# Products of zeros in TensorE's thinly filled steps of a selective scan

## The chip, the cores and the metric

The kernel runs on one core of one Trainium2 chip. Its time is the device time of one execution in microseconds (us); the figure that counts is the median of several runs. One further execution is recorded by the hardware profiler, and all views below are of that one.

## The reference

Four layers work on four images of 64 x 64 positions with 96 channels. Layers 0 and 1 are selective scans over the image, layers 2 and 3 are attention without softmax and a quantized feed-forward block. Nearly all the time goes into layers 0 and 1. There, after a group norm, an input projection and a depthwise 3 x 3 convolution, the 192 inner channels are read in K = 4 orders, and for each order and each of N = 16 states a recurrence runs along the 4096 positions:

```python
def step(h, inp):
    u_t, dt_t, B_t, C_t = inp
    h = jnp.exp(dt_t[..., None] * A) * h + (dt_t * u_t)[..., None] * B_t[:, :, None, :]
    y = jnp.einsum('bkdn,bkn->bkd', h, C_t)
    return (h, y)
```

The sums over the 16 states, plus a skip term, are added up over the four orders; a layer norm, a gate and an output projection follow.

## The kernel before

**Tiling.** Two images are worked on at a time. A *phase* is one layer for one pair of images, four in all. A phase has 16 *blocks* (four reading orders, four parts of TB = 1024 positions each). A block has 48 *tiles*: two groups `g`, three parts `j` of 64 channels, and eight steps `n` in each group. That is 3072 tiles. Tile `n` belongs to image `n % 2` and holds two neighbouring states of it, one in each half of the 128 partitions, for 64 channels and 1024 positions. So the 16 values of `n` are eight pairs of states for each of the two images.

**The order of the work.** For PE, DVE, ACT and POOL the order of the instructions is the order in which the program writes them (`manual_schedule`). A loop over steps `i` writes, in each step, pieces of several tiles, so that the engines work on neighbouring tiles at once. Only the queue of transfers on SP is ordered by the framework's planner. The loop's heart is:

```python
if 0 <= i - 3 < end and tiles[i - 3][3] % GN == GN - 1:
    flush(i - 3)
if 0 <= i - 2 < end and tiles[i - 2][3] % 2:
    gather(i - 2)
if 0 <= i + 2 < end:
    row(i + 2)
if 0 <= i < end:
    scan(i)
```

**The parts of a tile** (lines of the profile before):

- `begin` (L652): POOL multiplies `du` with a row of B that was copied to all partitions, for the five states of `POOL_N`. For the other states, ACT takes the exponential of the decay (L669) here.
- `row` (L662): for the states outside `POOL_N`, PE writes the row of B to all partitions of a PSUM tile `psB`, as two products of 128 x 512 in bf16. There are two `psB` buffers.
- `product` (L676): DVE multiplies `psB` with `du`.
- `scan` (L684): DVE runs the recurrence over 1024 positions.
- `weigh` (L695): POOL multiplies the states with a row of C.
- `gather` (L727): in every second step PE adds two tiles (one of each image) into the sum over states `psY`; the operand `fold` adds the two halves of partitions. These are four fp32 products of 64 x 512, each of which is two matmuls in the records.
- `resume` (L718): at the first tile of a group of eight, PE puts the earlier sum (or the skip term) into `psY`; it opens the sum. The last gather of the group closes it, and `flush` (L739, L743) copies it out on ACT.

There is one `psY` tile, and six `flow` buffers `f` that hold decays and then weighted states.

**Beside the scan.** In the same loop, `advance()` takes the next piece of other work: the convolution of the coming phase (`conv_pieces`, L289 on PE), the norm, gate and projection of the phase just done (`tail_pieces`, L360 to L442), and the preparation of the next block (L543, L565, L569). These use two small PSUM tiles `psM`. After the last tile, layers 2 and 3 follow.

Of the kernel before, what the change touches and what calls it, by code (L numbers as in the profile page):

```python
# [15 lines left out]
C = 96  # L16
# [11 lines left out]
NG = 2  # L28
GN = N // NG
MANUAL = {mybir.EngineType.PE, mybir.EngineType.DVE, mybir.EngineType.Activation, mybir.EngineType.Pool}  # L30
POOL_N = (1, 4, 7, 10, 13)


@with_exitstack
def kernel(ctx: ExitStack, tc: tile.TileContext, ins, out, layers=(0, 1, 2, 3)):
# [72 lines left out]

    minus = wp.tile([96, 2 * N], BF16, tag="minus", name="minus")
    nc.vector.tensor_scalar_mul(minus, m32[0:96], -1.0)  # L110


    def per_channel(name, cols, src, tag):
# [98 lines left out]
    def conv_pieces(w, xin, xc, zg, done):  # L212

        norms = []

        def part_of(n):
            xb = wide([C, T], "xb")
            nc.sync.dma_start(xb, xin[n // NT][:, n % NT * T : (n % NT + 1) * T])
            return xb

        xbs = [part_of(n) for n in range(3)]
        yield False
        yield False
        for i in range(2):
            stats = small([C, NT, 6], "gst")
            for t in range(NT):
                if t:
                    yield False
                nc.vector.bn_stats(stats[:, t, :], xbs.pop(0))
                if i * NT + t + 3 < 2 * NT:  # L230
                    xbs.append(part_of(i * NT + t + 3))
            mv = small([C, 2], "gmv")
            nc.vector.bn_aggr(mv, stats)
            yield False
            pm = psM([C, 1])
            nc.tensor.matmul(pm, gmat, mv[:, 0:1], start=True, stop=True)
            yield True
            mean = small([C, 1], "gmean")
            nc.vector.tensor_copy(mean, pm)
            dev = small([C, 1], "gdev")  # L240
            nc.vector.tensor_sub(dev, mv[:, 0:1], mean)
            nc.vector.tensor_mul(dev, dev, dev)
            nc.vector.tensor_add(dev, dev, mv[:, 1:2])
            yield False
            pv = psM([C, 1])
            nc.tensor.matmul(pv, gmat, dev, start=True, stop=True)
            yield True
            t = small([C, 1], "grs")
            nc.vector.tensor_scalar_add(t, pv, 1e-5)
            scale = small([C, 1], f"gscale{i}")  # L250
            nc.gpsimd.tensor_tensor(scale, t, mhalf[0:C, 0:1], ALU.pow)
            yield False
            shift = small([C, 1], f"gshift{i}")
            nc.vector.scalar_tensor_tensor(shift, mean, -1.0, scale, ALU.mult, ALU.mult)
            norms.append((scale, shift))
        if "join" in w:
            w.pop("join")()
        rows = T // HW

        def load(t):  # L260
            pads = []
            for i in range(2):
                r0, r1 = t * rows - 1, (t + 1) * rows + 1
                lo, hi = max(r0, 0), min(r1, HW)
                pad = wide([C, rows + 2, HW + 2], "pad")
                nc.vector.memset(pad[:, :, 0:1], 0.0)
                nc.vector.memset(pad[:, :, HW + 1 : HW + 2], 0.0)
                if lo > r0:
                    nc.vector.memset(pad[:, 0, 1 : HW + 1], 0.0)
                if hi < r1:  # L270
                    nc.vector.memset(pad[:, rows + 1, 1 : HW + 1], 0.0)
                inner = pad[:, lo - r0 : hi - r0, 1 : HW + 1]
                nc.sync.dma_start(inner, xin[i][:, lo * HW : hi * HW].rearrange("p (r c) -> p r c", c=HW))
                pads.append((pad, inner))
            return pads

        done.append(now[0])
        coming = load(0)
        for t in range(NT):
            pads, coming = coming, None  # L280
            yield False
            for i in range(2):
                nc.scalar.activation(pads[i][1], pads[i][1], AF.Identity, bias=norms[i][1], scale=norms[i][0])  # L283
            yield False
            for j in range(J):
                px = psM([128, T])
                for tap in range(9):
                    for i in range(2):
                        nc.tensor.matmul(  # L289
                            px[64 * i : 64 * i + 64], w["wf"][:, tap, 64 * j : 64 * j + 64],  # L290
                            pads[i][0][:, tap // 3 : tap // 3 + rows, tap % 3 : tap % 3 + HW],
                            start=(tap == 0), stop=(tap == 8),
                        )
                    yield MORE if tap < 8 else True
                xo = thin([128, T], "xo")
                nc.scalar.activation(xo, px, AF.Silu, bias=w["cb"][:, j, :])
                pz = psM([128, T])
                for i in range(2):
                    nc.tensor.matmul(
                        pz[64 * i : 64 * i + 64], w["wz"][:, 64 * j : 64 * j + 64],  # L300
                        pads[i][0][:, 1 : 1 + rows, 1 : 1 + HW], start=True, stop=True,
                    )
                zo = thin([128, T], "zo")
                nc.scalar.activation(zo, pz, AF.Silu)
                nc.sync.dma_start(xc[:, j, t * T : (t + 1) * T], xo)
                nc.sync.dma_start(zg[:, j, t * T : (t + 1) * T], zo)
                if j == J - 1 and t + 1 < NT:
                    coming = load(t + 1)
                if j == J - 1:
                    done[0] += 1  # L310
                yield False

    def tail_pieces(w, units, y, zg, xin, xout, tokens):
# [11 lines left out]
        for t in units:  # L325
# [31 lines left out]
            for q in range(2):  # L357
                pt = psM([128, 2, D])
                for j in range(J):
                    nc.tensor.matmul(  # L360
                        pt[:, :, 64 * j : 64 * j + 64], yu[:, j, q * 128 : (q + 1) * 128], ident, start=True, stop=True
                    )
                if q:
                    statistics(0, pts)
                pts = pt
                yield True
# [50 lines left out]
            if tokens:  # L417
                xo = thin([128, 2, 2, C], "xn")
                pos = []
                for i in range(2):  # L420
                    half = slice(64 * i, 64 * i + 64)
                    pos.append(psM([128, 2, 128]))
                    for q in range(2):
                        tok = slice(q * 128, (q + 1) * 128)
                        o = pos[i][:, q, 0:C]
                        nc.tensor.matmul(o, xr[:, i, tok], ident[0:C, 0:C], start=True, stop=False)
                        for j in range(J):
                            nc.tensor.matmul(o, zu[half, j, tok], w["ow"][half, j, :], start=False, stop=(j == J - 1))  # L428
                    yield True
                for i in range(2):  # L430
                    nc.scalar.copy(xo[:, i], pos[i][:, :, 0:C])
# [2 lines left out]
            else:  # L434
                xo = thin([C, 2, U], "xn")
                pos = []
                for i in range(2):
                    half = slice(64 * i, 64 * i + 64)
                    pos.append(psM([C, U]))
                    nc.tensor.matmul(pos[i], ident[0:C, 0:C], xr[:, i, :], start=True, stop=False)  # L440
                    for j in range(J):
                        nc.tensor.matmul(pos[i], w["ow"][half, j, :], zu[half, j, :], start=False, stop=(j == J - 1))  # L442
                    yield True
                for i in range(2):
                    nc.scalar.copy(xo[:, i, :], pos[i])
# [55 lines left out]
    def prepare(ph, k, t):  # L501
# [38 lines left out]
        def project(s, j):  # L540
            if j == 0:
                pps.append(psM([76, T]))
            nc.tensor.matmul(  # L543
                pps[s], order[0][0][:, j, :], xs[j][:, halves[s]], start=(j == 0), stop=(j == J - 1)
            )

# [14 lines left out]
        def take(s, q):  # L561
            of = taken[s] = psM([2 * N, T])
            part = slice(0, 32 * q + 32)
            nc.tensor.matmul(of, ident[0 : 2 * N, 0 : 2 * N], rests[s][0 : 2 * N], start=True, stop=False)
            nc.tensor.matmul(of, minus[part], p["parts"][part, halves[s]], start=False, stop=True)  # L565

        def steps(s, j):
            pds.append(psM([128, T]))
            nc.tensor.matmul(  # L569
                pds[-1], order[0][1][64:76, j, :], rests[s][64:76], start=True, stop=True  # L570
            )

# [84 lines left out]
    def row(i):  # L657
        at, g, j, n = tiles[i]
        if n not in POOL_N:
            for s in range(2):  # L660
                ss = slice(s * T, (s + 1) * T)
                nc.tensor.matmul(  # L662
                    scanned[i][0][:, ss], sel[:, n, :], made[at]["parts"][:, ss], start=True, stop=True
                )

# [40 lines left out]
    def resume(i):  # L706
# [8 lines left out]
            parts = [(py[:, s * T : (s + 1) * T], old[:, s * T : (s + 1) * T]) for s in range(2)]  # L715
        banks = len(parts) * T // TB
        for m, (o, v) in enumerate(parts):
            nc.tensor.matmul(o, of, v, start=(m % banks == 0), stop=False)  # L718

    def gather(i):  # L720
        at, g, j, n = tiles[i]
# [2 lines left out]
        for s in range(2):  # L724
            ss = slice(s * T, (s + 1) * T)
            for e in range(2):
                nc.tensor.matmul(  # L727
                    py[64 * e : 64 * e + 64, ss], fold, two[e][:, ss],
                    start=False, stop=(n == g * GN + GN - 1),
                )  # L730

    def flush(i):

# [284 lines left out]
    with tc.manual_schedule(engines=MANUAL):  # L1018
# [27 lines left out]
        for i in range(-9, end + 4):  # L1046
# [7 lines left out]
                flush(i - 3)  # L1054
            if 0 <= i - 2 < end and tiles[i - 2][3] % 2:
                gather(i - 2)
            if 0 <= i + 2 < end:
                row(i + 2)
            if 0 <= i < end:
# [152 lines left out]
```

## Time and profile before

| what | value |
|---|---|
| median of three runs | 11160.67 us |
| lowest, highest | 11153.93, 11168.22 us |
| the profiled execution's own time | 11149.85 us |
| its span, first to last instruction | 11148.1 us |
| its mean granted clock of TensorE | 0.87 |
| 40 slices, each | about 279 us |

PE is TensorE's matmuls and PEld its weight loads; DVE is VectorE, ACT is ScalarE, POOL is GpSimd, and SP holds the queue of transfers. In the page's groups, the columns after the bar are the busy time of the group in us, the mean of one instruction in ns, and the engine's idle time just before these instructions, with what ended most of it. In the list of waits, a line says who waited for whom, for how many us in total, how often, and the longest. The clock is given in tenths in the slices and as a share in the tables of stretches. A line of the timeline gives start and duration in us, engine, line, operation, tiles and count, and in brackets the idle time before it with what ended it.

### The profile page before, as it was taken

Reading aid. Unit: us, or ns where it says so; the run is one execution under the profiler, and the core shown is the slowest. Engines: PE = TensorE matmul, PEld = TensorE weight load, DVE = VectorE, ACT = ScalarE, POOL = GpSimd, SP = SyncE. Lnnn points to the kernel's source line nnn. Section 1 sums busy time; section 2 is a strip of 40 time slices with the busy share of each in tenths; the row PEclk is TensorE's granted clock in tenths of the full one; section 3 lists DMA queues with packets and bytes.
Section 4 is the critical chain, followed back from the end, with each engine's and each line's share of the span. In section 5 each row is a group of like instructions: output and inputs, shape, how many; then the busy total and the mean of one; then the engine's idle time right before and its main releaser. Section 6 shows DMA issues by size and latency. Waiting matters only on the chain. (4 is left out here: it accounts for less than half of the span.)

```text
span 11148.1 us, 101994 instructions
## 1 busy us (share of the span) xinstructions
PE 8910.0 (80%) x30112; PEld 2880.5 (26%) x30112; DVE 9926.4 (89%) x6431; ACT 6423.1 (58%) x10575; POOL 10204.6 (92%) x5102
## 2 busy tenths in 40 slices
PE   7978888777777779887788878887778877778777
PEld 2222222111222212221222222222222322222365
DVE  3898999999999889989999999999999999999846
ACT  3656556554566646665566656665466655555576
POOL 3989999999999889999999999999999999999846
PEclk8989999888888889998888889998888888888877
DMA  5679976897578885798666656665556565556410
GB/s 134 158 141 162 141 160 157 145 134 136 149 171 151 140 151 149 157 159 132 138 169 157 157 146 169 164 159 143 149 157 156 155 149 148 143 137 159 122 33 22
DMA packets 1848188, 1604.57 MB, mean 144 GB/s; under 512 B 1412298, under 2 KB 1482892, under 8 KB 1847628
## 3 DMA queue, kind: packets, MB, share of 16 engines
q1 hardware_dynamic: 1847628, 1598.04, 66.1%
q8 instruction: 237, 3.88, 0.2%
q14 instruction: 323, 2.65, 0.1%
HBM read 1008.37 MB, written 186.65 MB: 107 GB/s over the span
## 5 line engine op out<-in xcount | busy, mean ns | idle before, releaser
L695 POOL TENSOR_TENSOR f<-f,crep 128x1024 f32<-128x1024 f32 x3072 | 7158.9, 2354 | 395.9 <-DVE f L684 296.6
L727 PE MATMUL psY<-f,fold 128*64 128x512 f32 x12288 | 3795.1, 698 | 183.4 <-POOL f L695 182.8
L684 DVE TENSOR_TENSOR_SCAN f<-f,state,psB 128x1024 f32<-128x1024 f32 x1584 | 3717.8, 2347 | 206.2 <-ACT f L669 50.1
L669 ACT ACTIVATE f<-delta,L_a 128x1024 f32<-128x1024 f32 x2112 | 2406.5, 1145 | 903.9 <-PE psY L727 829.8
L676 DVE TENSOR_TENSOR psB<-psB,du 128x1024 f32<-128x1024 f32 x2112 | 2558.9, 1212 | 362.9 <-PE psB L662 322.1
L662 PE MATMUL psB<-spB,sel 96*128 96x512 bf16 x4224 | 1387.8, 414 | 1613.5 <-DVE f L684 1599.0
L652 POOL TENSOR_TENSOR f<-du,brep 128x1024 f32<-128x1024 f32 x960 | 2265.7, 2360 | 127.2 <-PE psY L727 29.4
L684 DVE TENSOR_TENSOR_SCAN f<-psB,state,f 128x1024 f32<-128x1024 f32 x720 | 1676.7, 2329 | 76.8 <-POOL f L652 50.3
L727 PEld LDWEIGHTS psY<-f,fold 128*64 128x64 f32 x12288 | 974.9, 154 | 2525.3 <-issue 1806.8
L690 ACT COPY state<-f 128x1 f32<-128x1 f32 x2304 | 429.7, 188 | 2065.8 <-DVE f L684 2056.7
L669 ACT ACTIVATE psB<-delta,L_a 128x1024 f32<-128x1024 f32 x960 | 1070.2, 1115 | 696.0 <-DVE f L684 636.1
L684 DVE TENSOR_TENSOR_SCAN f<-f,psB 128x1024 f32<-128x1024 f32 x528 | 1208.3, 2288 | 57.6 <-ACT f L669 5.9
L662 PEld LDWEIGHTS <-sel 96*128 96x128 bf16 x4224 | 271.3, 99 | 3320.4 <-DVE f L684 2163.7
L289 PE MATMUL psM<-pad,wf 96*64 96x512 f32 x3456 | 901.4, 623 | 36.0 <-ACT pad L283 28.9
L684 DVE TENSOR_TENSOR_SCAN f<-psB,f 128x1024 f32<-128x1024 f32 x240 | 545.6, 2273 | 102.9 <-ACT psB L669 60.0
L718 PE MATMUL psY<-ysum,ident 128*128 128x512 f32 x768 | 554.5, 862 | 98.3 <-ACT ynew L743 86.7
L585 POOL TENSOR_TENSOR xs<-delta,xs 128x1024 f32<-128x1024 f32 x192 | 452.7, 2358 | 95.0 <-ACT delta L582 95.0
L569 PE MATMUL psM<-proj,dtw 12*128 12x512 f32 x768 | 455.2, 686 | 0.0
L543 PE MATMUL psM<-xs,xp 128*76 128x512 f32 x768 | 414.7, 651 | 5.5 <-DMA xs<-xcd 4.2
L718 PE MATMUL psY<-yold,ident 128*128 128x512 f32 (+2 forms) x960 | 370.6, 526 | 42.2 <-ACT ysum L739 26.7
L289 PEld LDWEIGHTS psM<-pad,wf 96*64 96x64 f32 x3456 | 221.4, 138 | 501.0 <-issue 422.6
L743 ACT COPY ynew<-psY 128x1024 f32<-128x1024 f32 (+2 forms) x312 | 242.4, 818 | 171.5 <-PE psY L727 171.5
(149 smaller groups left out, 6644.6 us busy)
## 6 DMA issues: line engine op xcount, KB each, us to landing
crep<-bc SPq DMA_DIRECT2D x2048, 256.0 KB, 4.8
delta<-delta SPq DMA_DIRECT2D x768, 256.0 KB, 4.8
du<-xs SPq DMA_DIRECT2D x768, 256.0 KB, 6.2
brep<-bc SPq DMA_DIRECT2D x640, 256.0 KB, 4.9
yd<-ynew SPq DMA_DIRECT2D x192, 512.0 KB, 7.8
xraw<-xcd SPq DMA_DIRECT2D x144, 512.0 KB, 8.5
yold<-yd SPq DMA_DIRECT2D x144, 512.0 KB, 8.9
xcd<-xo SPq DMA_DIRECT2D x96, 256.0 KB, 3.0
```

The costliest lines, as they stand in the source:

```text
L289: nc.tensor.matmul(px[64 * i : 64 * i + 64], w["wf"][:, tap, 64 * j : 64 * j + 64], pads[i][0][:, tap // 3 : tap // 3 + rows, tap % 3 : ta ...
L569: nc.tensor.matmul(pds[-1], order[0][1][64:76, j, :], rests[s][64:76], start=True, stop=True)
L585: nc.gpsimd.tensor_mul(xs[j], deltas[j], xs[j])
L652: nc.gpsimd.tensor_mul(f[:, 1:], made[at]["dus"][j][n % 2], reps[at, 0, n])
L662: nc.tensor.matmul(scanned[i][0][:, ss], sel[:, n, :], made[at]["parts"][:, ss], start=True, stop=True)
L669: nc.scalar.activation(out, made[at]["deltas"][j][n % 2], AF.Exp, scale=W[phases[ph][0]]["a"][:, k, j, n // 2 : n // 2 + 1])
L676: nc.vector.tensor_mul(scanned[i][0], scanned[i][0], made[at]["dus"][j][n % 2])
L684: nc.vector.tensor_tensor_scan(f[:, 1:], a, bu, 0.0 if t == 0 else states[at - 1][:, c : c + 1], ALU.mult, ALU.add)
L690: nc.scalar.copy(states[at][:, c : c + 1], f[:, TB : TB + 1])
L695: nc.gpsimd.tensor_mul(f[:, 0:TB], f[:, 1:], reps[at, 1, n])
L718: nc.tensor.matmul(o, of, v, start=(m % banks == 0), stop=False)
L727: nc.tensor.matmul(py[64 * e : 64 * e + 64, ss], fold, two[e][:, ss], start=False, stop=(n == g * GN + GN - 1),)
```

## The change

A function `multiply` stands in front of the matmuls of most places. It issues the same matmul and adds to a running count `work[0]` how long the product takes on the array at full clock: 1/2400 us for each column, four times that in fp32, half of it where the output has 64 partitions or fewer. The matmuls of the layers 2 and 3 and the transposes in the tails are not counted.

In each step, between `gather` and `row`, a new function `warm(i - 2)` compares the count since its last call with `BUSY` = 2.2 us. What is missing is filled with products of 128 x 512 in bf16, whose stationary operand is a tile of zeros and whose moving operand is a part of the constant `sel`. They are added to the sum over states of that tile, with neither start nor stop, so that they change nothing in it. Where that sum isn't open (the first tile of a group of eight, whose `resume` comes at the end of the step) or has just been closed (the last tile), nothing is issued. The count is carried to the next step: the missing part, up to 2.2 us, as credit, and what exceeds 2.2 us as debt.

The diff, cut to its core:

```diff
+BUSY = 2.2
...
+    work = [0.0]
+    zeros = wp.tile([96, 128], BF16, tag="zeros", name="zeros")
+    nc.vector.memset(zeros, 0.0)
+
+    def multiply(out, lhsT, rhs, start, stop, **kw):
+        cols = 1
+        for n in out.shape[1:]:
+            cols *= n
+        work[0] += cols / 2400 * (4 if rhs.dtype == F32 else 1) * (0.5 if out.shape[0] <= 64 else 1.0)
+        nc.tensor.matmul(out, lhsT, rhs, start=start, stop=stop, **kw)
...
         if n not in POOL_N:
             for s in range(2):
                 ss = slice(s * T, (s + 1) * T)
-                nc.tensor.matmul(
+                multiply(
                     scanned[i][0][:, ss], sel[:, n, :], made[at]["parts"][:, ss], start=True, stop=True
                 )
...
+    def warm(i):
+        at, g, j, n = tiles[i]
+        py = sums.get((at, g, j))
+        spare = min(BUSY - work[0], BUSY)
+        work[0] = -spare
+        if py is None or n % GN == GN - 1:
+            return
+        while work[0] <= -T / 2400:
+            multiply(py[:, 0:T], zeros, sel[:, 0:4, :], start=False, stop=False)
...
             if 0 <= i - 2 < end and tiles[i - 2][3] % 2:
                 gather(i - 2)
+            if 0 <= i - 2 < end:
+                warm(i - 2)
             if 0 <= i + 2 < end:
                 row(i + 2)
```

The same replacement of `nc.tensor.matmul` by `multiply` is made in the group norm, the convolution, the tails, the preparation of a block, `resume` and `gather`.

More of the change, by code (lines that the diff above doesn't have):

```diff
@@ L235, in conv_pieces @@
             pm = psM([C, 1])
-            nc.tensor.matmul(pm, gmat, mv[:, 0:1], start=True, stop=True)
+            multiply(pm, gmat, mv[:, 0:1], start=True, stop=True)
             yield True
@@ L245, in conv_pieces @@
             pv = psM([C, 1])
-            nc.tensor.matmul(pv, gmat, dev, start=True, stop=True)
+            multiply(pv, gmat, dev, start=True, stop=True)
             yield True
@@ L298, in conv_pieces @@
                 for i in range(2):
-                    nc.tensor.matmul(
+                    multiply(
                         pz[64 * i : 64 * i + 64], w["wz"][:, 64 * j : 64 * j + 64],
@@ L359, in tail_pieces @@
                 for j in range(J):
-                    nc.tensor.matmul(
+                    multiply(
                         pt[:, :, 64 * j : 64 * j + 64], yu[:, j, q * 128 : (q + 1) * 128], ident, start=True, stop=True
@@ L425, in tail_pieces @@
                         o = pos[i][:, q, 0:C]
-                        nc.tensor.matmul(o, xr[:, i, tok], ident[0:C, 0:C], start=True, stop=False)
+                        multiply(o, xr[:, i, tok], ident[0:C, 0:C], start=True, stop=False)
                         for j in range(J):
-                            nc.tensor.matmul(o, zu[half, j, tok], w["ow"][half, j, :], start=False, stop=(j == J - 1))
+                            multiply(o, zu[half, j, tok], w["ow"][half, j, :], start=False, stop=(j == J - 1))
                     yield True
@@ L439, in tail_pieces @@
                     pos.append(psM([C, U]))
-                    nc.tensor.matmul(pos[i], ident[0:C, 0:C], xr[:, i, :], start=True, stop=False)
+                    multiply(pos[i], ident[0:C, 0:C], xr[:, i, :], start=True, stop=False)
                     for j in range(J):
-                        nc.tensor.matmul(pos[i], w["ow"][half, j, :], zu[half, j, :], start=False, stop=(j == J - 1))
+                        multiply(pos[i], w["ow"][half, j, :], zu[half, j, :], start=False, stop=(j == J - 1))
                     yield True
@@ L542, in project @@
                 pps.append(psM([76, T]))
-            nc.tensor.matmul(
+            multiply(
                 pps[s], order[0][0][:, j, :], xs[j][:, halves[s]], start=(j == 0), stop=(j == J - 1)
@@ L563, in take @@
             part = slice(0, 32 * q + 32)
-            nc.tensor.matmul(of, ident[0 : 2 * N, 0 : 2 * N], rests[s][0 : 2 * N], start=True, stop=False)
-            nc.tensor.matmul(of, minus[part], p["parts"][part, halves[s]], start=False, stop=True)
+            multiply(of, ident[0 : 2 * N, 0 : 2 * N], rests[s][0 : 2 * N], start=True, stop=False)
+            multiply(of, minus[part], p["parts"][part, halves[s]], start=False, stop=True)
         def steps(s, j):
             pds.append(psM([128, T]))
-            nc.tensor.matmul(
+            multiply(
                 pds[-1], order[0][1][64:76, j, :], rests[s][64:76], start=True, stop=True
@@ L661, in row @@
                 ss = slice(s * T, (s + 1) * T)
-                nc.tensor.matmul(
+                multiply(
                     scanned[i][0][:, ss], sel[:, n, :], made[at]["parts"][:, ss], start=True, stop=True
@@ L717, in resume @@
         for m, (o, v) in enumerate(parts):
-            nc.tensor.matmul(o, of, v, start=(m % banks == 0), stop=False)
+            multiply(o, of, v, start=(m % banks == 0), stop=False)
     def gather(i):
@@ L726, in gather @@
             for e in range(2):
-                nc.tensor.matmul(
+                multiply(
                     py[64 * e : 64 * e + 64, ss], fold, two[e][:, ss],
```

## The prediction

> **What bounds the kernel now.** I read the busy times and slices of the page first, then its costliest groups, then the table of stretches, then the waits, and last the timeline around one long wait.
>
> ```profile
> span 11148.1 us, 101994 instructions
> PE 8910.0 (80%) x30112; PEld 2880.5 (26%) x30112; DVE 9926.4 (89%) x6431; ACT 6423.1 (58%) x10575; POOL 10204.6 (92%) x5102
> PEclk8989999888888889998888889998888888888877
> L695 POOL TENSOR_TENSOR f<-f,crep 128x1024 f32<-128x1024 f32 x3072 | 7158.9, 2354 | 395.9 <-DVE f L684 296.6
> L727 PE MATMUL psY<-f,fold 128*64 128x512 f32 x12288 | 3795.1, 698 | 183.4 <-POOL f L695 182.8
> L662 PE MATMUL psB<-spB,sel 96*128 96x512 bf16 x4224 | 1387.8, 414 | 1613.5 <-DVE f L684 1599.0
> ```
>
> POOL is the bound, with DVE close behind. POOL's own work is fixed: 3072 weighings of 2354 ns, 960 products of 2360 ns (L652), 192 inputs of 2358 ns (L585), together 9877 us. What the change can move is only POOL's idle time. TensorE is busy for 80%, at a granted clock of 0.87: the clock record has two values only, full for 8209 us and half for 2903 us. The next question is whether half clock costs POOL anything.
>
> ```profile
> 3627.00:3906.00 279.00, 216.64 (x616) 67.38 (x616) 232.78 (x134) 167.59 (x304) 242.31 (x110) 0.82 0.85 139
> 7254.00:7533.00 279.00, 247.91 (x852) 68.87 (x850) 265.78 (x158) 170.70 (x238) 275.95 (x121) 0.94 0.64 165
> 9207.00:9486.00 279.00, 200.66 (x569) 55.88 (x566) 265.15 (x147) 143.47 (x226) 273.73 (x120) 0.84 0.56 140
> 9486.00:9765.00 279.00, 211.37 (x608) 59.42 (x606) 268.55 (x148) 147.31 (x247) 276.09 (x120) 0.86 0.62 153
> DVE psB L676 <- PE psB L662: 322.1, 242, 13.6
> POOL f L695 <- DVE f L684: 296.6, 212, 26.1
> ```
>
> In the stretches, columns are length, busy PE, PEld, DVE, ACT, POOL, clock, DMA, GB/s. In the plain scan from 9207 to 9765 the clock is 0.84 to 0.86, and yet POOL works 273.7 and 276.1 of 279 us: there is almost nothing to win where the clock is low and nothing else runs. POOL idles where tails or convolutions of other images run beside the scan. The two waits show how: DVE waits for the broadcast row that PE writes (322 us in all), and POOL then waits for DVE's scan. In the trace, 117 row waits of over 1 us between 300 and 10450 us sum to 254 us, and POOL's idle time from 4 us before to 8 us after each sums to 234 us: a late row is passed on to POOL at 0.92.
>
> ```profile
> 2743.83 3.78 PE L718 MATMUL psY<-ysum,ident 128*128 128x512 f32 x4 [4.51 <-ACT ynew L743]
> 2747.54 2.45 PE L727 MATMUL psY<-f,fold 128*64 128x512 f32 x8
> 2749.92 0.60 PE L662 MATMUL psB<-spB,sel 96*128 96x512 bf16 x2
> 2750.56 1.23 DVE L676 TENSOR_TENSOR psB<-psB,du 128x1024 f32<-128x1024 f32 x1 [2.79 <-PE psB L662]
> ```
>
> Here the resume (L718) started 4.5 us late, ran at half clock for 3.78 us, the gather after it 2.45 (1.94 at full clock elsewhere), and the row came 2.79 us late to DVE.
>
> **The change part by part.** *Calls through multiply, memset of zeros:* no instruction is altered; one DVE memset at the start, under 1 us. ACT's and POOL's orders are the same instruction for instruction, DVE's apart from that memset. SP's queue shows moves at 444 of 5796 transfers, nearly all of copies by a few places. The longest are six loads of xraw, 32 places later in the last sweep; in the trace before, such a place is about 50 us later (9549 to 9598), still some 20 us before the permuting copies read it (9620), against 8.5 us from issue to landing. I cost it at nothing; if that cover went, ACT would stand still in front of the copy. Bounds: 10 us either way.
>
> *The zeros.* The changed program holds 3269 products of 128x512, each behind its own weight load. The row (L662) has the same shape of work; a pair takes 0.60 us in the timeline, which I read as two of 0.21 us and about 0.17 us of drain, so one zero product costs 0.213 us at full clock, 697 us in all. The load (98 ns, PEld) runs beside the product before it.
>
> *Where they stand.* They lie in 468 runs, most of 8, 10 or 12. No run lies in the first image pair before its last block, nor in most of the blocks with convolution: the count `work` also carries excess on without limit, to 153 us in the first sweep, and no zero is issued until it is paid back. So the stretches concerned are about 2600 to 4060, 5200 to 6700 and 7800 to 10500 us, and in the first two only in part. A step that may not issue (first and last of a group of eight) keeps its credit: so 2 and 10 zeros meet without a row between, just after the resume.
>
> *Loss.* I laid each run over the trace of before: PE's idle gap in front of the matmul that follows covers it first, then the slack between the end of the next row and the DVE product that reads it. The gaps cover 462 us and the rows' slack most of the other 231 us. What is left is 42 us of later rows, in 61 runs, if all run at full clock, and 62 us if the 30 runs that start at half clock run at half. The worst are the 12 zeros in front of the row at 2749.92 above, where DVE already waits: 2.4 us more, and again at 5395 and 7945. At 0.92 these ends are 39 and 57 us; I take 46, nearer to the first as few runs start at half clock. Queued behind each run on PE are the row, then gather and tail products; for the row DVE waits, for the gather ACT's next exponential, for the tail ACT.
>
> *Gain.* Row waits of over 0.4 us in these stretches sum to 169 us, but for only 36 us of them a run of zeros lies between 1.5 and 16 us earlier, so that it could have kept the clock up. Most of the waits follow steps that hold no zeros. At 0.92 that is 33 us at most, nothing at least; as about half the time before such waits was at half clock already and lateness has other parts (PE waiting for ACT), I take 17. Faster gathers could save a little of POOL's waits for buffers besides, at most 15 us.
>
> *Two rules weighed.* The clock record runs in windows of 3.41 us. Of windows at full clock whose matmuls (less 0.165 us of drain each) filled 35 to 40%, 94% were followed by half clock; at 45 to 50%, 12%. The Trainium skill, "TensorE: Matmul & The Clock Gate", says under The HAM clock gate that half clock comes after an idle window, and under Terms puts the penalty at the time below full clock times the share missing, here one half. That would make 2903 x 0.5 = 1451 us to win; the trace has 322 us of DVE waiting for rows at any clock, so the trace decides, and partly filled windows do lose the clock. Against the change speaks the same page, Packing small matmuls, What overlaps and what doesn't: matmuls are strictly first in, first out. By it every zero in front of a row counts, 231 us after the gaps; the rows' slack in the trace leaves 42.
>
> *Sum.* 46 - 17 = +29 us. The profiled execution took 11149.85 us, 1.75 over its span; with 29 it is 11179. The median of the runs is 11160.67, 10.8 above it, so the time shown should be 11190.
>
> **The rivals.** *The clock pays (faster).* Laying the zeros into the windows, with half clock below 42% filled, the share of half clock falls by some 7 points in the tails and 17 in the last plain scan, mean clock near 0.89. If that cures all 36 us (-33), the buffer waits (-15), and rows that are earlier leave only half of the loss (+20), the sum is -28: 11133 us. It decides from some 50 us of cured row waits on, more than lie behind zeros; for it speaks that many late rows follow a resume and gather at half clock, against it that zeros are banned in just those steps.
>
> *It cancels.* Gain and loss within 22 us of each other, near 11165 us. For it speaks that POOL idles just 8 us of 558 in the plain scan, where most zeros of the last sweep lie.
>
> *The change doesn't do what it says.* If a product with zero weights does not count as work for the clock, half clock stays, runs there cost double, and only the loss of 57 us remains, with the queue order's 10 perhaps: 11218 to 11228 us. No row of before shows such a product.
>
> **How the numbers follow.** A measurement of this kernel can tell about 0.2%, 22 us. Chances: forecast, zeros late in front of rows, 0.40; no effect on the clock 0.10; cancelling 0.28; clock pays 0.22. So slower 0.50, same 0.28, faster 0.22. The forecast's own range is 11170 to 11218. The wider range reaches down to 11118, where the faster case has some luck with the queue order, and up to 11235, for both bounds of loss and queue together and a remainder for runs that meet on PE.
>
> **What would show it.** Right: zeros about 697 us of PE busy time; clock near 0.89; DVE's wait for rows at 330 to 370 us, POOL's busy time unchanged within 10 us, its idle time up about 30; the row at the turn of the block near 2750 us later by 2 us or more. Wrong: DVE's row wait under 290 us, or a clock of 0.95 with POOL less idle in the tails; or the row wait unchanged and SP or ACT the new releaser.

## The result, and the profile after

The changed kernel takes 11153.93 us (median of 20 runs, 11138.74 to 11178.0), the kernel before, run beside it, 11171.22 us (20 runs). The ratio is 0.9985, 95% interval 0.9978 to 0.9991: 17 us faster (10 to 25), where 29 us slower was forecast. It is less than the 0.2% that the prediction called measurable in a few runs; 20 runs on each side separate it from nothing.

Lines move by some 15 to 27 in the changed program, and all matmuls that go through `multiply` now stand under L125. So go by tiles: the weighing is L710 (was L695), POOL's product of du L667 (L652), DVE's product L691 (L676), the scan L699 (L684). The page of the changed kernel, its busy times, clock, and costliest groups that bear on the steps:

```profile
span 11141.9 us, 108575 instructions
...
PE 9371.0 (84%) x33381; PEld 3137.8 (28%) x33381; DVE 9923.3 (89%) x6432; ACT 6429.0 (58%) x10575; POOL 10210.0 (92%) x5102
...
PEclk9989999888999889998898989998899899999877
...
L710 POOL TENSOR_TENSOR f<-f,crep 128x1024 f32<-128x1024 f32 x3072 | 7166.0, 2358 | 412.0 <-DVE f L699 315.8
...
L667 POOL TENSOR_TENSOR f<-du,brep 128x1024 f32<-128x1024 f32 x960 | 2269.7, 2364 | 111.2 <-PE psY L125 31.9
...
L125 PE MATMUL psY<-sel,zeros 96*128 96x512 bf16 x3269 | 795.8, 384 | 0.0
```

The zeros are there, 3269 of them, and PE stands idle ahead of none. PE is busy 461 us longer although the zeros alone occupy 796: the rest of its work got shorter, because the mean clock rose from 0.87 to 0.897 (half clock 2903 us before, 2299 after). POOL's busy time is the same within 6 us. Its idle time before the weighing rose from 396 to 412, that before its product of du fell from 127 to 111. The two groups share one engine, so a wait can move from one to the other; their sum is the figure to read, and it is 523 us in both records. The group of before that the prediction doesn't show:

```profile
L652 POOL TENSOR_TENSOR f<-du,brep 128x1024 f32<-128x1024 f32 x960 | 2265.7, 2360 | 127.2 <-PE psY L727 29.4
```

Both are records of fast executions (11149.85 and 11143.67 us, 21 and 10 below their medians), so they are 6 us apart where the medians are 17. A difference of that size says little: the first zero comes at 2644 us, and yet POOL is 10 us ahead of before at the same instruction some 660 us after the start.

The waits, and the windows that stood in the prediction:

```profile
DVE psB L691 <- PE psB L125: 316.9, 228, 11.6
POOL f L710 <- DVE f L699: 315.8, 217, 26.1
```

```profile
3627.00:3906.00 279.00, 236.71 (x728) 74.45 (x725) 237.24 (x136) 171.67 (x309) 244.81 (x112) 0.85 0.83 138
9207.00:9486.00 279.00, 241.49 (x826) 77.93 (x824) 265.93 (x147) 144.14 (x226) 274.43 (x120) 0.93 0.56 141
9486.00:9765.00 279.00, 238.16 (x825) 75.77 (x821) 269.08 (x149) 148.98 (x248) 277.58 (x121) 0.96 0.62 155
```

The clock in the plain scan went from 0.84 and 0.86 to 0.93 and 0.96, and POOL's busy time there from 273.7 and 276.1 to 274.4 and 277.6 us of 279. That is the small gain that so large a rise of the clock brings where nothing else runs. DVE's wait for rows went from 322 to 317 us, where 330 to 370 was forecast. POOL's wait for the scan rose in the same record, from 297 to 316 us.

The turn of a block near 2750 us, in the timeline of the changed kernel:

```profile
2742.14 3.76 PE L125 MATMUL psY<-ysum,ident 128*128 128x512 f32 x4 [4.49 <-ACT ynew L768]
...
2745.82 1.94 PE L125 MATMUL psY<-f,fold 128*64 128x512 f32 x8
...
2747.70 2.76 PE L125 MATMUL psY<-sel,zeros 96*128 96x512 bf16 x12
...
2750.30 0.59 PE L125 MATMUL psB<-spB,sel 96*128 96x512 bf16 x2
...
2750.93 1.23 DVE L691 TENSOR_TENSOR psB<-psB,du 128x1024 f32<-128x1024 f32 x1 [4.84 <-PE psB L125]
```

Twelve zeros stand back to back between gather and row, and DVE waits 4.84 us where it had waited 2.79. The row is 2.05 us later; 2.4 was forecast. So one part of the forecast loss is real, and the total still has the other sign.

To see both sides I matched the 2112 rows of the two traces by number and compared DVE's idle time just before its product, whatever ended it:

| rows | number | before | after |
|---|---|---|---|
| with zeros since the row before ("in front") | 447 | 42.8 us | 66.1 us |
| - of these, just after a resume (the *turn*) | 154 | 22.4 us | 45.6 us |
| - of these, elsewhere | 293 | 20.4 us | 20.5 us |
| with zeros in front of one of the five rows before | 517 | 116.5 us | 87.8 us |
| with none near | 1148 | 203.6 us | 203.4 us |

The zeros cost 23 us of DVE waiting at the rows that they stand in front of, all of it at the turn, and they save 29 us at the rows that follow within some steps. The rows far from zeros don't change in sum.

The saving goes with the clock. For each of the 517 rows I compared the mean clock in the 6 us before DVE began to wait. At 99 of them it is over 0.1 higher than before, and their waits fell from 24.7 to 1.6 us, which is 23 of the 29; at 34 it is lower, and their waits rose by 3.9. Far from zeros the clock varies too from one execution to the next: 104 rows with a higher clock waited 36.5 us less, 108 with a lower one 42.7 us more. So a row's wait goes with its clock far more than the total shows, though row by row this is a correlation.

### The profile page after: what moved, and what is told of

It is laid out like the page before. It is cut to its first block, busy times and chain, and to the rows that moved or that the text cites. A ratio compares the mean times of both kernels' runs of the same rounds, so it can differ in the third digit from the quotient of the medians.

```text
span 11141.9 us, 108575 instructions
## 1 busy us (share of the span) xinstructions
PE 9371.0 (84%) x33381; PEld 3137.8 (28%) x33381; DVE 9923.3 (89%) x6432; ACT 6429.0 (58%) x10575; POOL 10210.0 (92%) x5102
## 5 line engine op out<-in xcount | busy, mean ns | idle before, releaser
L710 POOL TENSOR_TENSOR f<-f,crep 128x1024 f32<-128x1024 f32 x3072 | 7166.0, 2358 | 412.0 <-DVE f L699 315.8
L699 DVE TENSOR_TENSOR_SCAN f<-f,state,psB 128x1024 f32<-128x1024 f32 x1584 | 3717.1, 2347 | 211.9 <-ACT f L684 56.4
L125 PE MATMUL psY<-f,fold 128*64 128x512 f32 x12288 | 3609.4, 671 | 130.2 <-POOL f L710 129.2
L684 ACT ACTIVATE f<-delta,L_a 128x1024 f32<-128x1024 f32 x2112 | 2406.5, 1145 | 883.1 <-PE psY L125 788.4
L691 DVE TENSOR_TENSOR psB<-psB,du 128x1024 f32<-128x1024 f32 x2112 | 2556.2, 1210 | 357.3 <-PE psB L125 316.9
L667 POOL TENSOR_TENSOR f<-du,brep 128x1024 f32<-128x1024 f32 x960 | 2269.7, 2364 | 111.2 <-PE psY L125 31.9
L125 PE MATMUL psB<-spB,sel 96*128 96x512 bf16 x4224 | 1349.6, 403 | 1211.4 <-DVE f L699 1198.9
L699 DVE TENSOR_TENSOR_SCAN f<-psB,state,f 128x1024 f32<-128x1024 f32 x720 | 1676.2, 2328 | 85.3 <-POOL f L667 50.7
L125 PEld LDWEIGHTS psY<-f,fold 128*64 128x64 f32 x12288 | 939.5, 149 | 2356.1 <-issue 1754.2
L684 ACT ACTIVATE psB<-delta,L_a 128x1024 f32<-128x1024 f32 x960 | 1070.2, 1115 | 698.0 <-DVE f L699 683.5
L699 DVE TENSOR_TENSOR_SCAN f<-f,psB 128x1024 f32<-128x1024 f32 x528 | 1208.1, 2288 | 58.1 <-ACT f L684 5.9
L125 PEld LDWEIGHTS <-sel 96*128 96x128 bf16 x4224 | 277.4, 98 | 2739.8 <-DVE f L699 1669.8
L125 PE MATMUL psM<-pad,wf 96*64 96x512 f32 x3456 | 896.9, 621 | 42.2 <-ACT pad L298 32.6
L125 PE MATMUL psY<-sel,zeros 96*128 96x512 bf16 x3269 | 795.8, 384 | 0.0
L125 PE MATMUL psY<-ysum,ident 128*128 128x512 f32 x768 | 555.3, 863 | 98.3 <-ACT ynew L768 86.7
L699 DVE TENSOR_TENSOR_SCAN f<-psB,f 128x1024 f32<-128x1024 f32 x240 | 545.4, 2273 | 99.5 <-ACT psB L684 56.3
L125 PE MATMUL psM<-proj,dtw 12*128 12x512 f32 x768 | 460.8, 694 | 0.0
L125 PEld LDWEIGHTS <-zeros 96*128 96x128 bf16 x3269 | 304.4, 99 | 535.4 <-issue 224.7
L125 PE MATMUL psM<-xs,xp 128*76 128x512 f32 x768 | 406.9, 641 | 5.2 <-DMA xs<-xcd 3.8
L125 PE MATMUL psY<-yold,ident 128*128 128x512 f32 (+2 forms) x960 | 368.9, 524 | 42.3 <-ACT ysum L764 25.5
```

The lines of the kernel that those rows point to most:

```text
L125: nc.tensor.matmul(out, lhsT, rhs, start=start, stop=stop, **kw)
L667: nc.gpsimd.tensor_mul(f[:, 1:], made[at]["dus"][j][n % 2], reps[at, 0, n])
L684: nc.scalar.activation(out, made[at]["deltas"][j][n % 2], AF.Exp, scale=W[phases[ph][0]]["a"][:, k, j, n // 2 : n // 2 + 1])
L691: nc.vector.tensor_mul(scanned[i][0], scanned[i][0], made[at]["dus"][j][n % 2])
L699: nc.vector.tensor_tensor_scan(f[:, 1:], a, bu, 0.0 if t == 0 else states[at - 1][:, c : c + 1], ALU.mult, ALU.add)
L710: nc.gpsimd.tensor_mul(f[:, 0:TB], f[:, 1:], reps[at, 1, n])
```

## The experiments

Each run is compared with runs of before that were taken with it. The ratio has a 95% interval in brackets, and the us beside it are worked out from the ratio; plain medians differ from them by up to 9 us. The medians of before lie at 11155.89, 11169.16 and 11170.52 us in the three sets of runs, so runs of different sets are compared by their ratios only. "Rows in front" and "within five" are the rows of the table above, at the same numbers, whatever the run does there.

**Zeros behind the row.** `warm` is called after `row` in each step.

```diff
-            if 0 <= i - 2 < end:
-                warm(i - 2)
             if 0 <= i + 2 < end:
                 row(i + 2)
+            if 0 <= i - 2 < end:
+                warm(i - 2)
```

> The same function warm, called behind row(i+2) instead of ahead of it; 3347 zeros. Theory A (zeros in front of a row make that row late, and this is the whole price; the clock's gain comes from elsewhere): DVE's wait for rows falls from 317 us to about 290, the clock stays near 0.90, and the time is some 20 us below the changed kernel's, 0.997 of before. Rival B (the zeros only move to the front of the next gather and row, and make those late instead): row wait 310 to 330 us, 0.9985 of before as in the changed kernel.

Measured: 1.0055 (1.0042 to 1.0068), 61 us slower than before, and both expectations missed. The clock is 0.89. The page's groups, then the waits of before and of this run:

```profile
L710 POOL TENSOR_TENSOR f<-f,crep 128x1024 f32<-128x1024 f32 x3072 | 7160.3, 2354 | 428.8 <-DVE f L699 316.1
...
L667 POOL TENSOR_TENSOR f<-du,brep 128x1024 f32<-128x1024 f32 x960 | 2265.4, 2360 | 172.3 <-PE psY L125 44.2
```

```profile
ACT f L669 <- PE psY L727: 829.8, 479, 6.0
...
ACT f L684 <- PE psY L125: 977.5, 511, 8.9
...
DVE psB L691 <- PE psB L125: 380.7, 323, 8.5
```

POOL's idle time before its two groups is 601 us against 523, DVE waits 381 us for rows, and ACT 978 us for gathers to free the buffer `f` (830 before). The timeline in the plain scan shows where the zeros lie:

```profile
9600.58 0.61 PE L125 MATMUL psB<-spB,sel 96*128 96x512 bf16 x2 [0.24 <-DVE f L699]
...
9601.02 2.32 PE L125 MATMUL psY<-sel,zeros 96*128 96x512 bf16 x10
...
9603.27 2.86 PE L125 MATMUL psY<-f,fold 128*64 128x512 f32 x8
...
9604.20 0.20 PEld L125 LDWEIGHTS psY<-f,fold 128*64 128x64 f32 x4 [0.74 <-POOL f L710]
```

Row, ten zeros and gather follow without a gap. In this step the rest of the gather waits for POOL too, so the view shows the order, and the cost is read from the sums above. Ahead of the row, the same zeros lie where PE waits for DVE anyway, as the next run shows. So the row's wait for a free `psB` is the cover, and behind the row that cover is lost. The rows in front lost little here (42.8 to 45.0 us), but those within five waited 158.9 us instead of 116.5: moving the zeros did move the loss, as rival B said, and made it larger.

**No zeros at the turn.** The steps n = 1, 2, 9, 10 count their zeros but don't issue them, so that all other zeros stay where they are.

```diff
         while work[0] <= -T / 2400:
-            multiply(py[:, 0:T], zeros, sel[:, 0:4, :], start=False, stop=False)
+            if n % GN not in (1, 2):
+                multiply(py[:, 0:T], zeros, sel[:, 0:4, :], start=False, stop=False)
+            else:
+                work[0] += T / 2400
```

> The zeros of steps n = 1, 2, 9, 10 (just after a resume) are counted but not issued; 2121 of 3269 remain, at the same places as in the changed kernel. Theory A: the seven long delays at block turns (2 to 3 us each) are gone, row wait about 295 us, clock near 0.89, 0.997 of before. Rival C (those zeros carry the clock over the turn of a group, where most late rows are): clock near 0.88, row wait back at 320 us, no gain left, 1.000 of before.

Measured: 0.9976 (0.9967 to 0.9986), 27 us faster than before. Clock 0.891. The rows in front are back at 43.7 us (42.8 before): the 154 at the turn fell to 14.8, the 293 that still have zeros stand at 28.9 against 20.4, where the narrow zeros below, which bring no clock, give 24.3. The rows within five keep most of their gain (95.1 against 116.5). Theory A holds in clock and time, though the row wait of 305 us lies between its 295 and the 320 of rival C; rival C falls, as the gain is kept. The waits, and the cover in the timeline of the plain scan:

```profile
DVE psB L691 <- PE psB L125: 305.1, 227, 17.1
POOL f L710 <- DVE f L699: 289.0, 204, 26.1
```

```profile
9586.32 1.94 PE L125 MATMUL psY<-f,fold 128*64 128x512 f32 x8
...
9588.19 2.33 PE L125 MATMUL psY<-sel,zeros 96*128 96x512 bf16 x10
...
9591.60 0.60 PE L125 MATMUL psB<-spB,sel 96*128 96x512 bf16 x2 [1.08 <-DVE f L699]
```

After ten zeros PE still idles 1.08 us until DVE's scan frees the `psB` of the row: these zeros cost the row nothing.

**Zeros only at the turn.** The condition turned round, `if n % GN in (1, 2)`: 1148 zeros.

> Only the zeros of steps n = 1, 2, 9, 10 are issued, 1148, at the places they have in the changed kernel. Theory A: the price without the gain, row wait 335 to 345 us, 1.001 of before. Rival C: the gain is kept, row wait 310 to 320 us, 0.998 of before.

Measured: 1.0013 (1.0003 to 1.0022), 14 us slower, as theory A expected. Clock 0.875. The waits:

```profile
DVE psB L691 <- PE psB L125: 345.3, 263, 12.0
```

The rows in front go from 42.8 to 75.7 us; those within five gain just 2.6. The 12 zeros after the resume at six turns in the tails, which had waits already, make each row 2.2 to 3.4 us later, 16.3 us in all (16.4 in the changed kernel, less than nothing where none are issued). The two halves of the change measured apart, -26.8 and +14.5 us, add up to -12 us, against -17 measured for the whole, well within the intervals.

**No debt.** What exceeds 2.2 us is dropped, so that zeros come in the first sweep and beside the convolutions too.

```diff
-        work[0] = -spare
+        work[0] = -max(spare, 0.0)
```

> What a step has above 2.2 us is no longer carried on as debt: 7626 zeros, in the first sweep and beside the convolutions too. Theory A: clock 0.93 or above; the first sweep's plain scan wins a few us, but beside the convolutions, where PE is busy 88 to 90% of the time and rows are already late, each run makes rows later: row wait 350 us or more, 1.002 to 1.006 of before. Rival D (the clock pays wherever it is raised): row wait below 290 us, 0.996 of before.

Measured: 1.0001 (0.9992 to 1.0009), with 7626 zeros at a clock of 0.932 (half clock 1520 us). The wait for rows:

```profile
DVE psB L691 <- PE psB L125: 335.2, 235, 16.5
```

Both expectations missed: no loss of 0.2% or more, no gain either. Row waits are 335 us, below the 350 of theory A; the rows in front take 66.5 us again, those with none near in the changed kernel 227 against 204, those within five 85.7 against 116.5. DVE's idle time before all rows is 17 us more than before, POOL's before its two groups 1 us more (524), so part of the lateness didn't reach POOL; why stays open. This is the clearest case of a clock that rises and a time that doesn't.

**No debt, and none at the turn.** Both edits together.

> No debt is carried, and the zeros of steps n = 1, 2, 9, 10 are counted but not issued: 4865 zeros. Theory A, with POOL's wait for freed buffers as a second gain: POOL's idle time before its products of du falls from 110 us to about 75, the row wait is 310 to 320 us (rows beside the convolutions still later by some 20 us, those at the turn no longer), 0.9975 of before. Rival D (full clock pays everywhere): row wait below 300 us, 0.996. Rival E (zeros beside convolutions cost what the clock gives there): 0.999.

Measured: 0.9943 (0.9931 to 0.9956), 11113.99 us, the fastest: 64 us by the ratio. It was expected at 0.9975; the gain is twice as large. POOL's idle time before its products of du, forecast at 75 us as a second gain, is 104. The waits for rows are those that rival D asked for, but the next run speaks against D's reason. The page, then the waits:

```profile
span 11111.3 us, 111721 instructions
...
PEclk9999999988999889998999989999999989998877
```

```profile
DVE psB L691 <- PE psB L125: 291.1, 220, 16.2
POOL f L710 <- DVE f L699: 289.6, 208, 26.1
```

Against the run without debt alone, leaving out the 2761 zeros at the turn brings 0.58% and lowers the row wait from 335 to 291 us, although the clock falls from 0.932 to 0.911. The rows in front are down from 66.5 to 48.3 us, those with none near in the changed kernel from 227 to 188.

**None beside the convolutions.** As the last, but with no zeros in the blocks that convolve.

```diff
+BESIDE = (*range(11), *range(24, 30), *range(40, 46))
...
-            if n % GN not in (1, 2):
+            if n % GN not in (1, 2) and at not in BESIDE:
```

> As the run without debt and without zeros at the turn, but none are issued in the blocks that convolve beside the scan (the first 11 blocks, and blocks 8 to 13 of the second and third sweep): 3568 zeros. Theory A: the gain in the first sweep's plain scan and in the tails without the loss beside the convolutions; row wait about 300 us, POOL's idle time before its products of du about 80 us, 0.997 of before. Rival D: 0.9985, behind the run that also fills beside the convolutions.

Measured: 0.9943 (0.9931 to 0.9955), clock 0.902, row wait 293 us (POOL's idle time before its products of du 113, where 80 was expected):

```profile
DVE psB L692 <- PE psB L126: 292.9, 243, 12.7
```

It is the same as with zeros beside the convolutions: there they neither help nor harm within the intervals (0.12% each way). So rivals D and E fall, and theory A was too low on the size. What the two runs win over the run with debt (0.9976) comes from zeros elsewhere: the first sweep's plain scan, the tails, and the steps after the convolutions. How it is shared among these stays open.

**Narrow zeros.** The 2121 zeros of the run with none at the turn, at the same places, 32 columns wide.

```diff
-                multiply(py[:, 0:T], zeros, sel[:, 0:4, :], start=False, stop=False)
+                nc.tensor.matmul(py[:, 0:32], zeros, sel[:, 0, 0:32], start=False, stop=False)
+            work[0] += T / 2400
```

> The 2121 zeros that stay when none are issued at the turn, at the same places, but 32 columns wide and not 512. Theory A (the gain is the clock): the clock stays at 0.87, row wait about 322 us, POOL's idle time before its products of du about 110 us, 1.000 of before. Rival F (the gain comes from another order of SP's transfers, or from PE being kept at work at all): 0.998 as with the wide ones, at a clock of 0.87.

Measured: 1.0001 (0.9993 to 1.001) against 0.9976 with the wide ones, as theory A expected. The page:

```profile
PEclk8989999888888889998888889998888888888877
...
L710 POOL TENSOR_TENSOR f<-f,crep 128x1024 f32<-128x1024 f32 x3072 | 7160.6, 2355 | 408.0 <-DVE f L699 307.5
...
L667 POOL TENSOR_TENSOR f<-du,brep 128x1024 f32<-128x1024 f32 x960 | 2266.8, 2361 | 110.8 <-PE psY L125 29.7
```

The mean clock is 0.869, as before, and the gain is gone: the instructions alone bring neither, the columns do. (The slices are those of before, digit for digit, but tenths are coarse: the next run has the same digits at 0.881.) Of rival F this run tries one half only. SP's transfers stand here nearly in the order of before (8 of 5794 elsewhere, by tile), where with the wide zeros 218 are elsewhere, so it doesn't try whether their order brings the gain. Three readings limit that: with the wide zeros DVE waits 17 us less for rows, in waits that end with PE's row and not with a transfer; POOL's waits that a transfer ended fell from 70 us before to 55, but to 60 in this run without a gain; and the saving goes row by row with the clock. A share of some us for the transfers isn't excluded.

One more thing is read here. POOL's idle time before its product of du is 111 us in this run, which gains nothing. So the fall of that row from 127 to 111 us in the changed kernel proves no gain; it lies within what one execution differs from another by.

**Behind the row, none at the turn.** The first and the second edit together.

> Zeros behind the row, with those of steps n = 1, 2, 9, 10 counted but not issued; 2293 zeros. Theory G (behind the row the zeros have no idle time to lie in: they run between a row and the next gather, and make each gather, the buffers that it frees and the next row some 2 us later): still slower, 1.003 to 1.005 of before, row wait above 345 us, ACT's wait for gathers above 900 us. Rival H (the slowdown of the run with zeros behind the row came from the turn of a group alone): 0.998 as with the zeros ahead of the row, row wait about 305 us.

Measured: 1.0089 (1.0075 to 1.0103), 99 us slower, at a clock of 0.881. The waits:

```profile
ACT f L684 <- PE psY L125: 999.0, 505, 8.9
...
DVE psB L691 <- PE psB L125: 389.6, 314, 11.3
```

Theory G holds in its signs (its size was put at half), rival H falls: behind the row it isn't the turn that hurts, and the waits point to the gather. With the turn's zeros the time was less (1.0055, clock 0.890), so behind the row those brought a gain; why was not tried.

## Why the prediction was wrong

**What held.** POOL's fixed work (9877 us is the sum of the groups' busy times; counts times means give 9950, as instructions overlap a little), the count and cost of the zeros (697 us of columns; the union of their records, 796 us with drain), the clock (near 0.89 forecast, 0.897 measured), the small gain in the plain scan, the chain from a late row to POOL, the places of the worst delays and their size: 2.4 us forecast near 2750, 2.05 measured, 2.67 and 2.92 at the other two turns named. That SP's changed order costs nothing was not tried: no run has that order without wide zeros.

**The step that failed: the loss.** It was put at 46 us, which is 50 us of later rows at 0.92. The matched rows show 23, and the zeros at the turn alone cost 14 us of time. The trace of before was laid under the zeros as if PE came to each place at the old time. Laid again, with 0.213 us for each zero, it gives 47 us of later rows: 33 at the turn and 14 elsewhere, where many delays come out at 0.6 to 0.9 us. Measured in the changed kernel are 23 at the turn and none elsewhere (20.4 to 20.5 us). The long delays came as forecast; the many small ones did not. The likely reason is that at a higher clock PE's work ahead of such a run ends earlier and the gap in front of the row grows. That part is argued, not tried by itself.

**The second term: the gain.** It was put at 17 us of time, by taking half of the 36 us of long row waits with zeros in front. The matched rows show 29 us at DVE for the changed kernel, and the zeros outside the turn alone bring 27 us (16 to 37). So most of that bound was realised, and halving it was the error. What brings the 10 us of those 27 beyond the 17 us of DVE's row waits that this run saves isn't settled; the interval is wide enough to hold none.

**The sign.** With the measured terms the prediction's own sum is 23 - 29 = -6 us at DVE: the sign is right, and the medians have -17 (10 to 25 faster). That the two records differ by 6 us as well is chance, as POOL's 10 us ahead of the first zero show. So some 11 us of the 17 are not traced to row waits. Both terms were mis-sized, by 27 us and by 11 at DVE, and each towards slower. The change was faster by its gain at rows that follow zeros, and a rival of the prediction, the clock that pays, had the right direction and reason; that its figure, -28, is near what the change brings without the zeros at the turn (-27) is luck, since it counted the turn's losses in.

**The rules.** The half-clock penalty is no guide here. The formula that the prediction took from the Trainium skill ("TensorE: Matmul & The Clock Gate", Terms) makes 1451 us of it, an estimate that stayed far off: 604 us less of half clock brought 17 us in the changed kernel, 925 us less brought 64 without debt and with nothing at the turn, and 1382 us less brought nothing where the turn was filled too. The order of issue decided the details, as first in, first out (the same page, What overlaps and what doesn't) would have it: nearly the same zeros ahead of the row (0.9976) or behind it (1.0089) differ by 1.1% of the time, 126 us.

## What to carry to other kernels

A filler that keeps TensorE's clock up was free here only where TensorE would have waited anyway: put it directly ahead of the instruction that waits, and leave it out where TensorE itself is late, here after the resume of a sum. A count of work doesn't see which of the two it is; the timeline does. A rise of the clock is no gain by itself (0.932 brought nothing, 0.902 brought 64 us): ask which other engine waits for TensorE, and sum up that wait, not the time at half clock. And a delay worked out on an old trace should be checked against the times that the change itself moves.

## What the runs showed of the hardware

Products with zero weights count as work for the clock: the mean went from 0.87 to 0.932 with 7626 of 512 columns, and not at all with 2121 of 32 columns. In the changed kernel, windows of 3.41 us at full clock in which the matmuls (less 0.165 us of drain each) filled 35 to 40% were nearly all followed by half clock (52 of 54), those at 40 to 45% in two thirds of cases (27 of 40), those at 45 to 50% in a fifth (15 of 79). Before, the same three were 93%, 40% and 11%: the boundary lies at some 40 to 45% filled in both.
